# Sums of x taken with its additions and squares on ScalarE, delta*x on GpSimd, and the values' products of four key tiles in one run

## The chip, the cores and the metric

The kernel runs on one core of a Trainium2 chip. The metric is device time in microseconds (us) from start to end of the program, as the median of several runs. A core has five engines, each with its own queue that runs in the order written: TensorE (PE in the profile: matrix products; its loads of the stationary operand are shown as PEld), VectorE (DVE), ScalarE (ACT), GpSimd (POOL) and SyncE (SP), which here issues the DMA transfers. [...]

## The reference

Sixteen sequences of 512 tokens with 256 features pass three blocks; each block is put on a layer normalisation (mean and variance over the 256 features) and added to x:

```
x = x + attention(layernorm(x))     # RMS norm, 16 heads of 16, causal softmax, output projection, plus the normed x
x = x + experts(layernorm(x))       # base + shared low rank + top 2 of 6 low-rank experts
x = x + state_space(layernorm(x))   # conv, silu, delta = softplus(.), h = exp(A*delta)*h + delta*x*B, y = C.h, gate, projection
x = x + experts(layernorm(x))       # as before, once more
```

Everything is fp32. The recurrence runs over 512 steps for 256 features x 16 states of every sequence.

## The kernel before, in words

Each sequence stays in one tile `x` of 128 partitions (tokens) x 4 token tiles x 256. Its work is written as a list of 376 operations, each with an engine, an estimated cost, the buffers it reads and writes, and a function that issues the instructions. `Plan.order` (lines 126 to 220) simulates the engines with those costs while the program is being built, and picks on each engine the ready operation with the lowest priority number whose buffers are free. A priority is `STARTS[sequence] + TURNS[operation]`, two tables written out at the top. The order found is the order in which all queues are written, so operations of several sequences (four `x` tiles) are interleaved. `OVER` is by how many us a piece of work may overrun the moment for which an engine is kept free for the scores; `port=True` keeps big GpSimd operations and some VectorE operations apart in the plan.

The four stages of a sequence:

- `normalised` (476 to 497): for each of four token tiles, VectorE's `bn_stats` and `bn_aggr` (L481, L482) give mean and variance; GpSimd turns them into a scale and a shift in four small operations (L487 to L490); ScalarE applies them (L494). It is called four times a sequence: ahead of attention, routing, scan and the second routing. `turned` (L505, L508) transposes the result on TensorE, with a copy by ScalarE.
- `attention` (538 to 671): heads are worked in four groups `j` of four heads, two groups making a pair `i`. For each pair, scores of every query tile (L566, with the mask added by L568) only give the rows' maxima (VectorE, L637). The scores are then computed again for every key tile with the maxima folded in, ScalarE takes the exponential (L585) into `pt0` to `pt3`, and TensorE weighs the values with them (L590: four products of 32 columns each run side by side in the array). Scores for both go through `sc`, one buffer of four PSUM banks. The weighted values `av` are copied (L596), transposed back (L601) and divided (L608, L609).
- `routed` (674 to 763): routing of the experts in small VectorE operations, and products.
- `scan` (766 to 884): convolution (L780), gate, softplus to delta (L812), delta*x (L817, VectorE); delta and delta*x go out to DRAM (L816, L819) and come back spread over the states (L849); GpSimd multiplies by B (L856), ScalarE makes the decay (L861) in a PSUM bank, VectorE runs the recurrence (L864), GpSimd multiplies by C (L867), TensorE sums the states (L874).

`project` (515 to 530) ends each stage: products (L474), and VectorE adds two token tiles of the result to x in one instruction (L528). All PSUM tiles other than `sc` share one tag, `one`, with four banks; each of `pt0` to `pt3` has one buffer.

Of the kernel before, what the change touches and what calls it, by code (L numbers as in the profile page):

```python
# [21 lines left out]
OVER, CHANGE = 2.3, 97.0  # L22
STARTS = (
    0, 149, 234, 338, 413, 521, 619, 700, 790, 888, 996, 1074, 1174, 1263, 1369, 1447,
)
TURNS = (
    322, 924, 785, 870, 705, 84, 602, 525, 716, 736, 780, 829, 935, 688, 816, 888, 551, 888, 569, 780, 1037,
    1058, 780, 1053, 1052, 703, 823, 720, 796, 729, 794, 743, 758, 752, 822, 761, 826, 825, 945, 858, 844,
    656, 460, 479, 710, 820, 765, 711, 797, 755, 722, 823, 826, 738, 806, 840, 1808, 856, 863, 744, 849,
    851, 744, 788, 833, 754, 788, 766, 751, 859, 885, 1705, 883, 866, 807, 1037, 1066, 872, 1095, 1116, 757,  # L30
    814, 758, 845, 775, 829, 775, 854, 787, 878, 778, 819, 785, 833, 801, 850, 564, 392, 477, 669, 771, 810,
    720, 849, 837, 723, 824, 834, 729, 799, 814, 1625, 859, 798, 753, 898, 878, 758, 869, 924, 763, 873,
    814, 774, 828, 887, 1728, 845, 870, 913, 1017, 867, 1025, 795, 747, 619, 606, 834, 836, 824, 854, 204,
    875, 859, 701, 653, 760, 785, 601, 885, 649, 900, 844, 1052, 761, 625, 294, 465, 645, 644, 492, 604,
    701, 765, 811, 782, 660, 0, 531, 800, 645, 687, 566, 570, 613, 641, 518, 510, 470, 703, 660, 743, 1034,
    946, 605, 616, 676, 882, 619, 1044, 680, 1060, 712, 805, 957, 1000, 1101, 663, 941, 1101, 623, 890,
    1153, 849, 783, 616, 695, 622, 701, 684, 886, 650, 959, 803, 1136, 745, 727, 871, 1195, 973, 1019, 873,
    1211, 928, 818, 818, 937, 1046, 783, 1096, 904, 1208, 761, 767, 840, 962, 673, 1117, 931, 1159, 919,
    869, 880, 1059, 1081, 860, 1141, 944, 1257, 903, 867, 907, 1191, 989, 1264, 959, 1209, 1026, 890, 917,
    932, 1162, 952, 1293, 1071, 1366, 917, 930, 1018, 1268, 989, 1331, 1144, 1482, 1193, 1207, 930, 961,  # L40
    1168, 1480, 1042, 1195, 1009, 1344, 962, 968, 1052, 1231, 1060, 1264, 1093, 1321, 1019, 995, 969, 1128,
    1304, 1126, 1316, 1047, 1366, 973, 998, 1084, 1144, 1062, 1295, 1240, 1372, 1060, 993, 1019, 1122, 1311,
    1039, 1297, 1013, 1390, 1064, 1037, 1188, 1297, 1133, 1352, 996, 1349, 1058, 988, 1069, 1158, 1353,
    1153, 1350, 1021, 1424, 1076, 1045, 1055, 1230, 997, 1317, 1028, 1427, 999, 1130, 1032, 1059, 1037,
    1031, 1050, 1016, 1108, 1187, 528, 1091, 1082, 1153, 1067, 1132, 1266, 1209, 1446, 1077, 1275, 1141,
    1558, 1308, 1166, 904, 1004, 1071, 1242, 1188, 1479, 1564, 1511,
# [17 lines left out]
class Op:  # L64
    __slots__ = ("eng", "cost", "lat", "fn", "bufs", "after", "left", "seq", "turn", "num", "table", "load", "port", "then", "stage")


class Plan:
# [15 lines left out]
    def op(self, eng, cost, fn, r=(), w=(), lat=None, table=None, load=0.0, also=(), port=False):  # L84
# [29 lines left out]
        o.port, o.then, o.stage = port, None, self.stage  # L114
# [11 lines left out]
    def order(self):  # L126
# [4 lines left out]
        free, busy, table, link, port = dict(self.places), {}, None, 0.0, False  # L131
# [9 lines left out]
        while True:  # L141
            for eng, heap in ready.items():
# [28 lines left out]
                if o.table is not None:  # L171
                    cost += 1.3 * (o.table != table)
                    table = o.table
                if until is not None and self.wanted(o, what):
                    del kept[eng]
# [48 lines left out]
def tile_block(ctx: ExitStack, tc: tile.TileContext, a: dict, out: bass.AP):  # L224
# [198 lines left out]
    for name, k in (("st", 6), ("mv", 2), ("nm", 1), ("rs", 1)):  # L423
        sizes[name] = (3, [P, NT, k])
# [37 lines left out]
    def act(n):  # L462
        return 0.2 + n / 1200.0
# [12 lines left out]
    def normalised(x, eps, part, into):  # L476

        st, mv, rs, nm, xh = sbuf("st"), sbuf("mv"), sbuf("rs"), sbuf("nm"), sbuf("xh" + part)
        for t in range(NT):
            def stats(t=t):  # L480
                nc.vector.bn_stats(st()[:, t, :], x()[:, t, :])  # L481
                nc.vector.bn_aggr(mv()[:, t, :], st()[:, t, :])  # L482

            op("DVE", 0.6, stats, r=[(x, t)], w=[(st, t), (mv, t)])

        def scales():
            nc.gpsimd.tensor_scalar(rs()[:, :, 0], mv()[:, :, 1], eps, 1.0, ALU.add, ALU.mult)  # L487
            nc.gpsimd.tensor_tensor(rs()[:, :, 0], rs()[:, :, 0], neg_half, ALU.pow)  # L488
            nc.gpsimd.tensor_scalar(nm()[:, :, 0], mv()[:, :, 0], -1.0, 0.0, ALU.mult, ALU.add)
            nc.gpsimd.tensor_tensor(nm()[:, :, 0], nm()[:, :, 0], rs()[:, :, 0], ALU.mult)  # L490

        op("POOL", 1.65, scales, r=[mv], w=[rs, nm], port=True)
        for t in range(NT):
            op("ACT", act(256) + 0.18, lambda t=t: nc.scalar.activation(  # L494
                xh()[:, t, :], x()[:, t, :], AF.Identity, bias=nm()[:, t, 0:1], scale=rs()[:, t, 0:1]
# [454 lines left out]
```

## Time and profile before

| | |
|---|---|
| median of 3 runs | 2063.27 us (2061.38 to 2065.82) |
| profiled execution, its own time | 2066.51 us |
| its span, first to last instruction | 2064.7 us |
| TensorE clock granted, mean | 0.954 |
| busy: TensorE / VectorE / GpSimd / ScalarE | 1801.9 / 1513.4 / 1371.1 / 1194.0 us |
| DMA moved | 316.35 MB, mean 153 GB/s |

The profile comes from one execution. A group of instructions has a line, an engine, an operation, the tiles written and read, the shapes, a count, the busy time in us, the mean of one in ns, and the engine's idle time just before them with what ended it. Busy TensorE time counts overlapping products once, but does not show the pauses between runs of different shape. A wait is put down to the instruction that released it last.

### The profile page before, as it was taken

What the parts mean: (1) busy time and instruction counts of PE and PEld (TensorE: products, weight loads), DVE (VectorE), ACT (ScalarE), POOL (GpSimd) and SP (SyncE); (2) the same over time, 40 slices, a digit from 0 to 9 for tenths busy, and PEclk for the clock granted to TensorE, in tenths of its full rate; (3) what the DMA queues carried; (4) which work ended last, traced back from release to release, by engine and by line L of the source; (5) the groups of instructions that cost most, each with busy time, mean ns of one, the idle gap of its engine ahead of it and who ended that gap; (6) DMA issues with size and microseconds to landing.
All of it is one profiled execution on the core that took longest, in us unless ns stands there. A gap on an engine that the chain in (4) does not pass through costs nothing. (4 is left out here: it accounts for less than half of the span.)

```text
span 2064.7 us, 34733 instructions
## 1 busy us (share of the span) xinstructions
PE 1801.9 (87%) x13253; PEld 953.8 (46%) x13253; DVE 1513.4 (73%) x2479; ACT 1194.0 (58%) x1685; POOL 1371.1 (66%) x814
## 2 busy tenths in 40 slices
PE   4788789999999999999999999999999999996455
PEld 2244344555455454545455454545554454544123
DVE  4335677878788787878788787878788787876563
ACT  2236556565666757565666667575666766564431
POOL 3001784949587685859597785859596785848693
PEclk8789899999999999999999999999999999998766
DMA  3000956848494866847494867849493957747791
GB/s 93 1 1 22 216 122 155 197 127 210 109 233 109 216 164 167 205 137 191 110 231 100 225 153 175 204 120 212 110 231 95 228 143 186 183 125 183 186 222 31
DMA packets 113064, 316.35 MB, mean 153 GB/s; under 512 B 17809, under 2 KB 36610, under 8 KB 112898
## 3 DMA queue, kind: packets, MB, share of 16 engines
q1 hardware_dynamic: 112194, 313.99, 62.5%
q8 instruction: 105, 1.72, 0.4%
q14 instruction: 61, 0.50, 0.1%
q10 hardware_dynamic: 704, 0.14, 0.0%
HBM read 287.87 MB, written 26.21 MB: 152 GB/s over the span
## 5 line engine op out<-in xcount | busy, mean ns | idle before, releaser
L864 DVE TENSOR_TENSOR_SCAN dd<-one,dd 128x512 f32<-128x512 f32 x512 | 607.9, 1212 | 185.2 <-ACT one L861 88.3
L856 POOL TENSOR_TENSOR dd<-dd,bc 128x1024 f32<-128x1024 f32 x256 | 603.6, 2361 | 194.0 <-DMA dd<-drows 156.8
L867 POOL TENSOR_TENSOR dd<-dd,bc 128x1024 f32<-128x1024 f32 x256 | 601.9, 2358 | 86.2 <-DVE dd L864 80.4
L637 DVE TENSOR_REDUCE negm<-sc 128x4 f32<-128x512 f32 (+3 forms) x256 | 380.4, 1486 | 154.0 <-PE sc L568 153.7
L861 ACT ACTIVATE one<-dd,am 128x512 f32<-128x512 f32 x512 | 344.3, 689 | 249.4 <-DVE dd L864 108.9
L585 ACT ACTIVATE pt<-sc 128x2048 f32<-128x2048 f32 (+3 forms) x256 | 316.3, 1235 | 189.0 <-PE sc L568 187.8
L487 POOL TENSOR_SCALAR rs<-mv 128x4 f32<-128x4 f32 x64 | 12.3, 193 | 364.2 <-DVE mv L482 361.4
L566 PE MATMUL sc<-qm,kT 32*128 32x512 f32 (+3 forms) x2048 | 214.1, 488 | 37.8 <-ACT pt L585 28.4
L566 PE MATMUL sc<-kT,qT 32*128 32x128 f32 (+3 forms) x2048 | 217.0, 494 | 30.5 <-DVE negm L637 25.9
L568 PEld LDWEIGHTS <-identb 128*128 128x128 bf16 x2048 | 117.4, 98 | 232.4 <-issue 217.2
L874 PE MATMUL one<-dd,ysel 128*32 128x512 f32 x1024 | 172.7, 633 | 55.5 <-POOL dd L867 46.4
L590 PE MATMUL one<-pt,vv 128*32 128x512 f32 (+3 forms) x2048 | 191.6, 449 | 8.1 <-DVE dd L864 7.9
L566 PEld LDWEIGHTS sc<-qm,kT 32*128 32x128 f32 x2048 | 80.9, 185 | 181.5 <-ACT pt L585 120.4
L474 PE MATMUL one<-base,xtR 128*128 128x256 f32 x512 | 139.5, 395 | 18.6 <-DVE dd L864 18.0
L566 PEld LDWEIGHTS sc<-kT,qT 32*128 32x128 f32 x2048 | 82.0, 187 | 156.8 <-DVE negm L637 63.3
L494 ACT ACTIVATE xhR<-x,nm,rs 128x256 f32<-128x256 f32 x192 | 99.4, 588 | 53.2 <-POOL nm L490 53.1
L528 DVE TENSOR_TENSOR x<-one,x 128x512 f32<-128x512 f32 x128 | 86.4, 675 | 34.7 <-PE one L474 34.5
L474 PEld LDWEIGHTS one<-base,xtR 128*128 128x128 f32 x512 | 94.5, 194 | 36.8 <-DVE dd L864 21.5
L481 DVE BATCH_NORM_STATS2 st<-x 128x6 f32<-128x256 f32 x256 | 103.7, 405 | 4.8 <-DMA x<-in_x_dram 4.1
L568 PE MATMUL sc<-mask_q,identb 128*128 128x128 bf16 x1024 | 103.7, 225 | 0.0
L568 PE MATMUL sc<-mask_k,identb 128*128 128x128 bf16 x1024 | 102.8, 224 | 0.0
L505 PE MATMUL one<-ident,xhR 128*128 128x128 f32 x384 | 61.9, 290 | 35.2 <-ACT xhR L494 27.7
(132 smaller groups left out, 2449.4 us busy)
## 6 DMA issues: line engine op xcount, KB each, us to landing
dd<-drows SPq DMA_DIRECT2D x512, 512.0 KB
x<-in_x_dram SPq DMA_DIRECT2D x16, 512.0 KB
drows<-dt SPq DMA_DIRECT2D x32, 256.0 KB
drows<-sg SPq DMA_DIRECT2D x32, 256.0 KB
bc<-brows SPq DMA_DIRECT2D x16, 512.0 KB
out_dram<-x SPq DMA_DIRECT2D x16, 512.0 KB
brows<-few SPq DMA_DIRECT2D x16, 64.0 KB
wo<-in_Wo_dram SPq DMA_DIRECT2D x2, 256.0 KB
```

The lines of the kernel that those rows point to most:

```text
L474: nc.tensor.matmul(o[:, lo:hi], lhsT=lhsT, rhs=rhs, start=n == 0, stop=n == len(todo) - 1)
L481: nc.vector.bn_stats(st()[:, t, :], x()[:, t, :])
L566: nc.tensor.matmul(sc()[:, g, 0:n], lhsT=lhsT(g), rhs=rhs(g), start=True, stop=False)
L568: nc.tensor.matmul(sc()[:, g, at : at + P], lhsT=identb, rhs=mask, start=False, stop=True)
L585: o.then = op("ACT", act(G * n), lambda pt=pt, sc=sc, n=n: nc.scalar.activation(pt(), sc()[:, :, 0:n], AF.Exp), r=[sc], w=[pt], table="exp")
L590: nc.tensor.matmul(av()[rows(g), kt * P : T], lhsT=vals()[:, kt, G * j + g, :], rhs=pt()[:, g, :], start=kt == 0, stop=kt == NT - 1,)
L637: o.then = op("DVE", dve(G * n), lambda t=t, n=n, sc=sc, nm=nm, s=s: nc.vector.tensor_reduce(nm()[:, t, :, 1 - s, 0:1], sc()[:, :, 0:n], A ...
L856: op("POOL", pool(1024), lambda dd=dd: nc.gpsimd.tensor_tensor(dd()[:, :, 1, :], dd()[:, :, 1, :], both(0), ALU.mult), port=True, r=[(bc, ...
L861: op("ACT", act(512) + 0.07, lambda i=i, k=k, dd=dd, dec=dec: nc.scalar.activation(dec(), dd()[:, i, 0, :], AF.Exp, scale=am[:, k + 4 * i ...
L864: op("DVE", 1.22, lambda i=i, dd=dd, dec=dec: nc.vector.tensor_tensor_scan(dd()[:, i, 1, :], dec(), dd()[:, i, 1, :], 0.0, ALU.mult, ALU.a ...
L867: op("POOL", pool(1024), lambda dd=dd: nc.gpsimd.tensor_tensor(dd()[:, :, 1, :], dd()[:, :, 1, :], both(1), ALU.mult), port=True, r=[(bc, ...
L874: nc.tensor.matmul(sums()[rows(g), :], lhsT=ysel[:, m, :], rhs=four[g]()[:, g % 2, 1, :], start=m == 0, stop=m == 3)
```

## The change

The diff does five things.

1. `project` gets an option `more`, true for three of the four stages. Where it is set, VectorE adds each token tile on its own with `scalar_tensor_tensor`, which also writes the sum over the features into `sums`; the last stage of a sequence keeps the old addition.
2. `normalised` takes these sums where it is given them (three of its four calls): GpSimd makes the negative mean of them, ScalarE squares x minus the mean with the sum of squares as accumulator output (into the tile `xh`, which the normalised values overwrite later), GpSimd makes scale and shift in three small operations.
3. delta*x moves from VectorE to GpSimd.
4. The values' products of the four key tiles of a head group, before issued one by one after each exponential, are issued in one run after the last of them. The plan holds all four `pt` buffers from the scores on until that run.
5. The planner's costs are replaced by others (several given in the diff), `OVER` and `CHANGE` get other values, a cost of 0.2 us is left out where two 32-column runs follow each other, and both tables of priorities are replaced, so the order of all queues is another one. The list has 367 operations a sequence.

```diff
-OVER, CHANGE = 2.3, 97.0
+OVER, CHANGE = 1.8, 98.0
 STARTS = (
-    0, 149, 234, 338, 413, 521, 619, 700, 790, 888, 996, 1074, 1174, 1263, 1369, 1447,
+    0, 250, 450, 689, 961, 1201, 1411, 1675, 1928, 2203, 2451, 2680, 2957, 3175, 3503, 3764,
 )
...
+                if eng == "PE":
+                    cost -= 0.2 * (o.mode is not None and o.mode == mode)
+                    mode = o.mode
...
+        else:
+            op("POOL", 0.25, lambda: nc.gpsimd.tensor_scalar(
+                mv()[:, :, 0], sums()[:, :, 0], -1.0 / D, 0.0, ALU.mult, ALU.add
+            ), r=[sums], w=[(mv, 0)], port=True)
+            for t in range(NT):
+                op("ACT", act(256) + 0.2, lambda t=t: nc.scalar.activation(
+                    xh()[:, t, :], x()[:, t, :], AF.Square, bias=mv()[:, t, 0:1], accum_out=mv()[:, t, 1:2]
+                ), r=[(x, t), (mv, 0)], w=[(xh, t), (mv, 1 + t)], also=[into])
+
+            def scales():
+                nc.gpsimd.tensor_scalar(rs()[:, :, 0], mv()[:, :, 1], 1.0 / D, eps, ALU.mult, ALU.add)
+                nc.gpsimd.tensor_tensor(rs()[:, :, 0], rs()[:, :, 0], neg_half, ALU.pow)
+                nc.gpsimd.tensor_tensor(nm()[:, :, 0], mv()[:, :, 0], rs()[:, :, 0], ALU.mult)
...
-        op("PE", 0.66, turn, r=[xh], w=[one], also=[xt, *also])
+        op("PE", 0.57, turn, r=[xh], w=[one], also=[xt, *also])
...
-            op("DVE", dve(512), add, r=[one], w=[(x, t), (x, t + 1)])
+            def add_sum(t=t, one=one):
+                for i in range(2):
+                    nc.vector.scalar_tensor_tensor(
+                        x()[:, t + i, :], one()[:, i * D : (i + 1) * D], 1.0, x()[:, t + i, :], ALU.mult, ALU.add,
+                        accum_out=sums()[:, t + i, 0:1],
+                    )
...
-            o = op("PE", pe(n, 1, 0.09) + 0.45, run, r=reads, w=[sc], also=[into])
+            o = op("PE", pe(n, 1, 0.0) + 0.5, run, r=reads, w=[sc], also=[into])
...
+            pts = [sbuf(f"pt{kt}") for kt in range(NT)]
...
-                def weigh(kt=kt, pt=pt, av=av, j=j):
+            def weigh():
+                for kt in range(NT):
                     for g in range(G):
                         nc.tensor.matmul(
-                            av()[rows(g), kt * P : T], lhsT=vals()[:, kt, G * j + g, :], rhs=pt()[:, g, :],
+                            av()[rows(g), kt * P : T], lhsT=vals()[:, kt, G * j + g, :], rhs=pts[kt]()[:, g, :],
                             start=kt == 0, stop=kt == NT - 1,
                         )
-                op("PE", pe(n, 1, 0.1), weigh, r=[pt, vals], w=[av], also=[avs])
+            op("PE", 2.2 + 0.2, weigh, r=pts + [vals], w=[av], also=[avs], mode="columns")
...
-            op("DVE", dve(512) + 0.1, lambda e=e: nc.vector.tensor_tensor(dx()[:, e, :], dt()[:, e, :], xc()[:, e, :], ALU.mult),
+            op("POOL", pool(512), lambda e=e: nc.gpsimd.tensor_tensor(dx()[:, e, :], dt()[:, e, :], xc()[:, e, :], ALU.mult),
                r=[(dt, e), (xc, e)], w=[(dx, e)], port=True)
...
-        routed(x)
-        scan(b, x)
-        routed(x)
+        sums = routed(x, sums, True)
+        sums = scan(b, x, sums)
+        routed(x, sums, False)
```

Of the table `TURNS`, which has one number for each operation of a sequence, the change gives these typical values (before, then after): attention's scores 700 to 860, then 1290 to 1870; the first routing's operations 290 to 1050, then 130 to 1200; the scan's products by B 680 to 1190, then 1030 to 2140.

## The prediction

> **What bounds the kernel now.** I read first the page of the kernel before: engine totals and the row of slices.
>
> ```profile
> span 2064.7 us, 34733 instructions
> ...
> PE 1801.9 (87%) x13253; PEld 953.8 (46%) x13253; DVE 1513.4 (73%) x2479; ACT 1194.0 (58%) x1685; POOL 1371.1 (66%) x814
> ...
> PE   4788789999999999999999999999999999996455
> ...
> PEclk8789899999999999999999999999999999998766
> ```
>
> TensorE is the busiest, saturated from about 300 us to 1850 us, thin at both ends. Next, busy times by stretches of one sequence's length (the rows of the same kind lie 115.5 us apart: outputs leave at 400, 515, 630 ... 1786 us). Columns: length, then busy us of each engine, TensorE's clock, DMA share.
>
> ```profile
> 0.00:115.00 115.00, 70.23 (x442) 32.80 (x443) 42.27 (x85) 27.87 (x37) 15.53 (x32) 0.78 0.16 42
> 115.00:231.00 116.00, 97.36 (x748) 49.42 (x746) 53.66 (x101) 60.09 (x78) 19.92 (x16) 0.94 0.24 60
> 231.00:346.00 115.00, 101.77 (x760) 52.99 (x752) 82.88 (x121) 67.22 (x96) 76.83 (x43) 0.96 0.59 140
> ...
> 1501.00:1617.00 116.00, 109.11 (x832) 58.46 (x836) 93.61 (x152) 74.57 (x107) 85.56 (x51) 1.00 0.71 170
> ...
> 1848.00:1950.00 102.00, 67.98 (x368) 37.16 (x368) 62.92 (x94) 51.57 (x72) 79.87 (x41) 0.82 0.77 184
> 1950.00:2064.70 114.70, 53.06 (x187) 27.89 (x185) 54.60 (x96) 27.69 (x46) 74.82 (x39) 0.67 0.59 138
> ```
>
> In the middle a sequence takes 115.5 us, of which TensorE is busy 109, VectorE 94, GpSimd 86, ScalarE 75. The 6.5 us left to TensorE are not free: I took the start of every product in the trace, grouped them into runs of one line and shape, and set a run's end at its last start plus its columns at the pace seen inside runs. That splits the span into 1610 us of streaming, 1514 changes of array shape (32-row scores, full products, 32-column products) at 95 ns each (median gaps 94 to 96 ns for every pair of shapes) = 144 us, and about 290 us of waiting: 77 before 300 us, 110 after 1800 us, 99 between (6.6 per 100 us). Per middle sequence: 98.5 streaming, 9.0 changes, 8.0 waiting. So the middle is TensorE's. Who ends its waits from 300 to 1800 us (total us, times, longest):
>
> ```profile
> PE sc L566 <- ACT pt L585: 18.3, 64, 0.4
> PE one L474 <- DVE dd L864: 16.7, 12, 1.4
> PE one L645 <- DVE dd L864: 9.2, 13, 0.9
> PE one L590 <- DVE dd L864: 7.4, 13, 0.6
> PE one L505 <- DVE dd L864: 6.6, 13, 0.5
> ```
>
> The last four, 40 us, have nothing to do with the scan's data: the scan reads a decay out of one of the four `one` banks of PSUM, and a product waits for that bank. PSUM banks are the second limit.
>
> The prices come from the groups kept apart by shape (busy us, mean ns, then idle before):
>
> ```profile
> L856 POOL TENSOR_TENSOR dd<-dd,bc 128x1024 f32<-128x1024 f32 x256 | 603.6, 2361 | 194.0 <-DMA dd<-drows 156.8 <-PE one L474 14.3 <-PE one L645 8.0
> L481 DVE BATCH_NORM_STATS2 st<-x 128x6 f32<-128x256 f32 x256 | 103.7, 405 | 4.8 <-DMA x<-in_x_dram 4.1
> L494 ACT ACTIVATE xhR<-x,nm,rs 128x256 f32<-128x256 f32 x192 | 99.4, 588 | 53.2 <-POOL nm L490 53.1
> L528 DVE TENSOR_TENSOR x<-one,x 128x512 f32<-128x512 f32 x128 | 86.4, 675 | 34.7 <-PE one L474 34.5
> L482 DVE BATCH_NORM_AGGREGATE mv<-st 128x2 f32<-128x6 f32 x256 | 46.6, 182 | 8.9
> L817 DVE TENSOR_TENSOR sg<-dt,xc 128x512 f32<-128x512 f32 x32 | 25.9, 809 | 8.6 <-ACT dt L812 8.6
> ```
>
> [...] L817 (both in SBUF) takes 809 ns against 675 for L528 (one in PSUM)[...]. [...] The trace's loads take 1283 ns.
>
> **The change part by part.** Sums are against the profiled execution: span 2064.7, its time 2066.5, 3.2 above the median of 2063.3; I carry the difference to the median.
>
> *Merged values' products.* Three of four separate L590 runs go from each of 64 head groups. Taking those 192 out of the recorded order leaves 1325 changes of shape for 1514: 189 x 0.095 = -18 us on the bounding engine, -1.1 a sequence. Streaming stays. The second effect: the bank `av` is now held from the first run of L590 to the end of its copy L596, 10.47 us on average; with one run it is 2.13 (1280 columns, two passes) + about 1.0 from run to copy + 0.58 = 3.7. That frees 4 x 6.8 = 27 us a sequence of 4 x 115.5 = 462 bank-us, 6%. Worth between 0 and the 40 us above; I take -15. The new wait: the run waits for the fourth exponential, with all of TensorE's queue behind it, and the next group's first scores wait until it has freed `pt0`. Scores hold their one buffer for 1165 of the 1500 middle us, so 22% is slack, and the other pair's maxima (L637) can use it; while the long run goes, TensorE works anyway. I take 0, with the uncovered case below.
>
> *Statistics.* 48 of 64 normalisations lose 4 x (405 + 182) ns: -112.7 us of VectorE. 96 additions of 675 ns become two of 256 elements with an accumulator. L780's form takes 748 ns at 512, so 748 - 256/0.96 = 0.48 at 256; the accumulator is between 0 and 0.18 (the smallest VectorE instructions), I take 0.06: 2 x 0.54 - 0.675 = +0.41, x 96 = +39. With delta*x gone (-26) VectorE drops by 100, 6.2 a sequence (94 to 88). ScalarE gains 192 squares, nearest L494 at 588 ns, upper end 0.77; at 0.65 +125, 7.8 a sequence (75 to 82). A table set without squares would add up to 48 x 1.28 = 62 to it; ScalarE would still have some 30 us a sequence. GpSimd has four small operations as before. None bounds; directly 0.
>
> *delta*x on GpSimd.* 32 x half of 2361 = +38 us, 2.4 a sequence (86 to 88). Behind it stand L856 and L867, for which the scans wait; its store on SP's queue stands ahead of the fetches L849. GpSimd has 27 us of slack a sequence: 0 in the middle.
>
> *Where the cover is gone: the tail.* After the last exponential (1864 us) 197 us follow with one sequence's work left. A normalisation's chain changes by: addition +0.4, two statistics -1.2, GpSimd's mean +0.3, four squares +2.4, so +2, and one more turn in GpSimd's queue of 0 to 2.4. Three of them and two delta*x (+0.4 each and a turn): +7 to +18; I take +9.
>
> *Order.* All priorities are replaced. The new costs sit on this trace: scores of 512 columns cost 1.35 in the new plan and 1.48 in the old, and the trace gives 0.93 + 0.24 + two changes = 1.36. Four transposes 0.57 for 0.66; the trace 0.46 + 0.1. The queues run in written order, so gaps are laid where they now belong. I read priorities by phase: before, attention stands near 800 and the scan near 1030 with sequences 98 apart (2.3 ahead); after, 1490 and 1800 with 250 apart (1.2 ahead), and the first routing far ahead at about 700. GpSimd's first L856 is at 215 us, 81 after the first attention's end; earlier scans fill the start. The waits that order can reach are 77 + 99 + 110. Bounds: -90 (a third of them) to +40. I take -36: about 12 at the start, 24 in the middle (1.7 a sequence), nothing at the tail, where the serial chain rules.
>
> Sum: -18 - 15 + 9 - 36 = -60; 2063 - 60 = 2003 us.
>
> **Rivals.** *Only the changes of shape.* Banks and order give nothing, the tail costs 9: -9 to -30, 2033 to 2054, centre 2045. For it: 93% use of TensorE's time in the middle is hard to better. Against: the 40 us of bank waits. *The score chain becomes the bound (slower).* If each merged run starts late and nothing fills the single `sc` buffer, every one of 4 per sequence keeps it idle 2.13 + 0.19 + about 1 = 3.4 us: 13.6 on 25.9 idle. Half of the present idle is only TensorE being elsewhere, 13; so the chain needs 89.7 + 13 + 13.6 = 116.3, plus queueing. It decides when more than about 4 us per merged run stay uncovered; at 5.0 the period is 118.5 to 119, 14 x 3.3 = +46, 2100 us. For it: today's next first exponential follows 1.6 to 3.5 us after the fourth in half of the joints. Against: the gap to beat includes q scores that are independent. *The order gains all*: -18 - 40 - 90 + 9 = 1925.
>
> **Numbers.** The likeliest case (1960 to 2032) 0.60; only shapes (2032 to 2059) 0.20; more gain, under 1960, 0.03; within 0.2% (4 us, about what a measurement of this kernel can tell) 0.03; slower 0.14, of which a third ends below 2070. So faster 0.83, same 0.03, slower 0.14. 1960 to 2070 leaves out 0.03 and about 0.09.
>
> **What would show it.** TensorE's changes of shape near 1325 and its middle waiting below 8 us a sequence; L590's runs of four key tiles at about 2.1 us; waits "PE one ... <- DVE dd" under 25 us; outputs 112 to 114 us apart; VectorE near 1415, ScalarE near 1320, GpSimd near 1410; squares near 0.65 us without more table loads; GpSimd's first big product before 200 us. Wrong if the first exponential of a group waits for the values' products and outputs are 117 us or more apart, or if the time after the last exponential grows well over 206 us.

## The result, and the profile after

The changed kernel takes 2127.62 us (2121.08 to 2135.48), the kernel before 2064.55 us in the same session: ratio 1.031, 95% interval 1.027 to 1.035. It is slower by 63 us; the forecast was 2003 us, faster. The profiled execution of the changed kernel took 2121.08 us, its span is 2119.3 us, 54.6 longer than the span before.

The page of the changed kernel: span, engine totals, two rows of the 40 slices.

```profile
span 2119.3 us, 35012 instructions
...
PE 1800.9 (85%) x13253; PEld 979.2 (46%) x13253; DVE 1400.3 (66%) x2351; ACT 1292.8 (61%) x2077; POOL 1410.8 (67%) x846
...
PE   4678888999989998998999999998999998986544
...
PEclk8779999999999999999999999999999999998756
```

The engine totals are those forecast (VectorE 1415, ScalarE 1320, GpSimd 1410), and TensorE is busy as long as before, 1801 us. But between 300 and 1850 us its row, before a string of nines, now has eights. Outputs leave at 383, 502, 619, 739 ... us, 119.3 apart where it was 115.5.

The same stretches of the changed kernel, one period of 119 us each and the end (length, then busy us of TensorE, its loads, VectorE, ScalarE and GpSimd, granted clock, DMA share, GB/s):

```profile
0.00:119.00 119.00, 70.83 (x461) 34.39 (x465) 42.17 (x85) 32.18 (x40) 15.53 (x32) 0.80 0.16 40
119.00:238.00 119.00, 99.11 (x776) 52.54 (x771) 46.97 (x94) 55.72 (x85) 15.90 (x15) 0.90 0.17 41
...
1553.00:1672.00 119.00, 110.93 (x816) 60.22 (x808) 84.31 (x143) 78.70 (x127) 85.34 (x51) 0.94 0.66 158
1918.00:2020.00 102.00, 55.64 (x260) 32.14 (x252) 52.61 (x106) 47.59 (x90) 74.96 (x44) 0.74 0.70 169
```

In a middle period TensorE is busy 111 of 119 us (109 of 116 before), VectorE, ScalarE and GpSimd 79 to 85, and TensorE's clock stands at 0.94, where the kernel before had 1.00 there.

Split as in the forecast, TensorE's span is now 1607 us of streaming (1610 before), 1318 changes of array shape at 95 ns (1514 before, so 18.6 us less), and 365 us of waiting (287 before). Streaming is counted at full pace, so what a lower clock costs is counted as waiting here. Streaming and shapes gain 21, waiting loses 78. By place: 79 us of waiting before 300 us (77), 164 between 300 and 1800 (99), 122 after (110). The middle is where it was lost; by the profile alone, TensorE is idle for 128 us of it (88 before). Who ends TensorE's waits there, in the changed kernel (us in all, times, longest):

```profile
PE sc L603 <- ACT pt L623: 95.2, 78, 2.3
PE sc L603 <- DVE qm L690: 10.1, 12, 0.8
PE one L529 <- ACT xhR L518: 4.7, 11, 0.7
PE one L702 <- DVE dd L904: 4.0, 11, 0.4
PE one L630 <- DVE dd L904: 3.2, 9, 0.4
```

The first row was 18.3 us before, with a longest wait of 0.4. The scores wait for an exponential to leave the single buffer `sc`. The waits for PSUM banks behind the recurrence (DVE dd, 40 us before) have nearly gone: 9.9 us with two smaller rows.

The new operations, as groups of the changed kernel (busy us, mean ns, then idle before):

```profile
L507 ACT ACTIVATE xhR<-x,mv 128x256 f32<-128x256 f32 x192 | 95.1, 497 | 89.3 <-POOL mv L503 89.3
L507 ACT ACTIVATION_READ_ACCUMULATOR xhR<-x,mv 128x1 f32 x192 | 36.0, 187 | 0.0
L558 DVE SCALAR_TENSOR_TENSOR x<-one,x 128x256 f32<-128x256 f32 x192 | 72.7, 416 | 55.7 <-PE one L480 55.7
L558 DVE DVE_READ_ACCUMULATOR x<-one,x 128x1 f32 x192 | 15.9, 83 | 0.0
L503 POOL TENSOR_SCALAR mv<-sums 128x4 f32<-128x4 f32 x48 | 9.3, 193 | 249.7 <-DVE x L558 249.7
L857 POOL TENSOR_TENSOR sg<-dt,xc 128x512 f32<-128x512 f32 x32 | 40.5, 1266 | 146.3 <-ACT dt L852 146.3
```

A square costs 497 + 187 = 684 ns on ScalarE, an added token tile 416 + 83 = 499 ns on VectorE: near the 650 and 540 of the forecast (whose 0.96 elements per ns on VectorE is also what L637 shows in the kernel before: 684 ns for 512 elements, 2285 for 2048). What had not been priced is that engines stop in their queues for these operations: in the whole run GpSimd stood 250 us at the mean and 146 us at delta*x (before, 364 us at the scales of L487).

### The profile page after: what moved, and what is told of

It reads as the page before. It is cut to its first block, busy times and chain, and to the rows that moved or that the text cites. A ratio compares the mean times of both kernels' runs of the same rounds, so it can differ in the third digit from the quotient of the medians.

```text
span 2119.3 us, 35012 instructions
## 1 busy us (share of the span) xinstructions
PE 1800.9 (85%) x13253; PEld 979.2 (46%) x13253; DVE 1400.3 (66%) x2351; ACT 1292.8 (61%) x2077; POOL 1410.8 (67%) x846
## 5 line engine op out<-in xcount | busy, mean ns | idle before, releaser
L603 PE MATMUL sc<-qm,kT 32*128 32x512 f32 (+3 forms) x2048 | 224.9, 511 | 133.1 <-ACT pt L623 113.4
L603 PEld LDWEIGHTS sc<-qm,kT 32*128 32x128 f32 x2048 | 85.2, 195 | 233.0 <-ACT pt L623 165.0
L503 POOL TENSOR_SCALAR mv<-sums 128x4 f32<-128x4 f32 x48 | 9.3, 193 | 249.7 <-DVE x L558 249.7
L630 PE MATMUL one<-pt,vv 128*32 128x512 f32 (+3 forms) x2048 | 168.5, 473 | 3.5 <-DVE dd L904 3.2
L507 ACT ACTIVATE xhR<-x,mv 128x256 f32<-128x256 f32 x192 | 95.1, 497 | 89.3 <-POOL mv L503 89.3
L857 POOL TENSOR_TENSOR sg<-dt,xc 128x512 f32<-128x512 f32 x32 | 40.5, 1266 | 146.3 <-ACT dt L852 146.3
L630 PEld LDWEIGHTS one<-pt,vv 128*32 128x32 f32 x2048 | 63.3, 117 | 100.6 <-issue 79.3
L558 DVE SCALAR_TENSOR_TENSOR x<-one,x 128x256 f32<-128x256 f32 x192 | 72.7, 416 | 55.7 <-PE one L480 55.7
L605 PE MATMUL sc<-mask_k,identb 128*128 128x128 bf16 x1024 | 108.1, 232 | 0.0
L570 POOL TENSOR_TENSOR x<-x,bo 128x1024 f32<-128x1024 f32 x32 | 75.5, 2361 | 44.1 <-ACT xhR L518 29.7
```

The source lines that it names most:

```text
L603: nc.tensor.matmul(sc()[:, g, 0:n], lhsT=lhsT(g), rhs=rhs(g), start=True, stop=False)
L605: nc.tensor.matmul(sc()[:, g, at : at + P], lhsT=identb, rhs=mask, start=False, stop=True)
L630: nc.tensor.matmul(av()[rows(g), kt * P : T], lhsT=vals()[:, kt, G * j + g, :], rhs=pts[kt]()[:, g, :], start=kt == 0, stop=kt == NT - 1,)
```

## The experiments

Each ratio is against runs of the kernel before on the same chip in the same session. The letters of the theories are set anew in each group.

### The parts one by one, in the order of the kernel before

In this group A is that the joined run takes from TensorE the work that stood between the scores; B is that the new order is what loses. The order recorded before was kept in all four, and only what is issued at a place was changed.

Values' products kept back until the fourth exponential, or until the tile that they read is needed again:

```diff
-                def weigh(kt=kt, pt=pt, av=av, j=j):
+                def weigh(kt=kt, pt=pt, av=av, j=j, late=late):
+                    late.append((kt, pt))
+                    held[kt] = late
+                    if kt == NT - 1:
+                        flush(late, av, j)
```

> The kernel before with its order kept; only the values' products are kept back on TensorE's queue until the last key tile's (or until the tile of weights they read is about to be overwritten), so they run together. Theory A (these products were what TensorE did while ScalarE read the scores, and keeping them back leaves it waiting): 2095 to 2135 us, waits of scores for the exponentials well over 60 us in the middle instead of 18. Theory B (the loss comes from the new order of all queues, the merging is a gain): 2040 to 2060 us, because some 150 changes of array shape at 95 ns are saved.

Measured: 2185.03 us, ratio 1.059 (1.057 to 1.061): slower as A says, and 50 us beyond A's range. TensorE's changes of shape fell to 1325, as forecast of the merged run, and yet it lost 121 us. TensorE's first wait in the middle of this run:

```profile
PE sc L571 <- ACT pt L583: 93.9, 110, 2.0
```

With nothing but the products moved, the scores' waits for exponentials rise from 18.3 to 93.9 us, almost the 95.2 of the change. So that new wait is made by the joined run; it is 76 of the 121 us. What stood between the scores can be seen in two timelines (start, length, engine and line, idle time before it), of the kernel before and of the change:

```profile
706.41 0.40 PE L568 MATMUL sc<-mask_k,identb 128*128 128x128 bf16 x4
706.74 0.85 PE L590 MATMUL one<-pt,vv 128*32 128x384 f32 x8
707.92 0.50 PE L566 MATMUL sc<-qm,kT 32*128 32x128 f32 x8 [0.33 <-ACT pt L585]
```

```profile
480.83 0.40 PE L605 MATMUL sc<-mask_k,identb 128*128 128x128 bf16 x4
482.34 1.19 PE L603 MATMUL sc<-qm,kT 32*128 32x384 f32 x8 [1.11 <-ACT pt L623]
```

Before, values' products follow the scores of one key tile (which end with the mask), then the next scores. In the change 56 of the 95.2 us of these waits begin right behind the mask: nothing stands between.

New statistics alone (additions with sums, mean by GpSimd, squares by ScalarE at the place of GpSimd's scales):

```diff
+                nc.gpsimd.tensor_scalar(mv()[:, :, 0], sums[0][:, :, 0], -1.0 / D, 0.0, ALU.mult, ALU.add)
+                for t in range(NT):
...
+                    nc.scalar.activation(junk, x()[:, t, :], AF.Square, bias=mv()[:, t, 0:1], accum_out=mv()[:, t, 1:2])
```

> The kernel before with its order kept; only the statistics are changed: sums with the additions, mean on GpSimd, squares on ScalarE, all issued where GpSimd's scales stood. Theories A and B: 2055 to 2075 us, no bound is touched. Theory C (the longer chain of each normalisation, through GpSimd twice and ScalarE twice, delays what feeds TensorE): 2085 us or more.

Measured: 2167.36 us, ratio 1.050 (1.048 to 1.052), 104 us lost, as theory C of this expectation has it. GpSimd's waits in the middle of this run, in the same columns:

```profile
POOL rs L494 <- ACT junk L493: 165.9, 37, 7.7
POOL mv L490 <- DVE x L543: 132.6, 13, 19.0
```

Before, GpSimd stopped once at a normalisation, 182.6 us in the middle. Now it stops for the additions and again for the squares, 298 us.

delta*x on GpSimd alone (the same call, `nc.gpsimd` for `nc.vector`):

> The kernel before with its order kept; only delta*x is issued on GpSimd at the same place. Theories A and B: 2060 to 2070 us. Theory C (GpSimd in series with the scan's feed): 2080 us or more.

Measured: 2063.40 us, ratio 0.9996 (0.9988 to 1.0004). No loss in this order, although GpSimd stands at delta*x for 151 us of the middle.

All three together, in the order before:

> The three parts together, in the order of the kernel before, so only the order of the queues differs from the kernel after. Theory A: 2100 to 2140 us, like the kernel after. Theory B: 2035 to 2070 us, 60 or more below the kernel after. Theory C: the sum of the losses of the two single runs, over 2100 us.

Measured: 2293.01 us, ratio 1.111 (1.109 to 1.113): 229 us, and 121 + 104 + 0 is 225. The losses add up. The order written for the changed program takes 165 of the 229 us back. B, that the new order is the loss, falls for the changed program; and in this order the forecast of 0 falls for two of the three parts.

### The parts undone, in the order of the change

If the joined run or the statistics were the loss in this order too, undoing one should give time back. Products of each key tile issued behind the next tile's scores where a PSUM bank was free:

```diff
-            op("PE", 2.2 + 0.2, weigh, r=pts + [vals], w=[av], also=[avs], mode="columns")
+            runs.append((op("PE", 2.2 + 0.2, None, r=pts + [vals], w=[av], also=[avs], mode="columns"), scores, piece, av))
...
+            for piece, kt in behind.get(i, []):
+                piece(kt)
```

> The kernel after with its order kept; only each key tile's values' products are taken out of the single run and issued on TensorE's queue behind the scores of the next key tile. Theory A (these products were what TensorE did while ScalarE read the scores): 2060 to 2090 us, the middle's waits of scores for exponentials fall from 95 to under 40 us, although 150 to 190 changes of array shape come back (+14 to +18). Theory B (the new order itself is what waits): 2125 to 2150 us, the waits stay and the changes of shape are added.

Measured: 2203.10 us, ratio 1.068 (1.066 to 1.071). Both theories missed; it is 75 us slower than the change. TensorE's first waits in the middle of this run:

```profile
PE sc L605 <- ACT pt L625: 63.4, 60, 2.0
PE sc L605 <- DVE negm L678: 48.9, 60, 1.6
```

The waits for exponentials fell from 95 to 63 us as A says, but scores that read row maxima now wait 48.9 us for VectorE, and the changes of shape are back at 1499. The order had been laid out for joined runs.

VectorE's statistics put back in place of GpSimd's mean, without squares, and then with the products apart as well:

> The kernel after with its order kept; only the statistics are as before (bn_stats and bn_aggr where GpSimd's mean stood, plain additions, no squares). If the new order has hidden the longer chain of the normalisation that cost 104 us in the old order: 2115 to 2150 us. If that chain still costs in the kernel after: under 2105 us.

> The two together in the order of the kernel after. Theory A with hidden statistics: the same as with the products apart alone, 2060 to 2100 us. If the statistics still cost: below 2050 us. Theory B: over 2115 us.

Measured: 2154.36 us, ratio 1.044 (1.042 to 1.046), and 2217.29 us, 1.074 (1.072 to 1.076). Undoing costs 27 and 90 us: the first is 4 us beyond the range for a chain that the new order hides, the second lies in B's range. In either direction, an operation changed or moved costs tens of us where the order of the queues was not made for it; only delta*x, in the old order, did not. A part alone in a foreign order therefore may overstate its own cost, and can't price the change.

### An order of its own for each program

So I looked for other starting times, priorities and weights for three programs, and ran one order of each. A is now that the loss is that of one poor order, B that it belongs to the operations. Only the two tables and the two weights change, here those of the changed program:

```diff
-OVER, CHANGE = 1.8, 98.0
+OVER, CHANGE = 1.89305, 1603.35
 STARTS = (
-    0, 250, 450, 689, 961, 1201, 1411, 1675, 1928, 2203, 2451, 2680, 2957, 3175, 3503, 3764,
+    0, 257, 364, 159, 882, 305, 573, 413, 1213, 736, 122, 1028, 607, 806, 989, 1490,
 )
```

> The changed program, every operation and cost as in the change, but with other starting times, turns and the two weights of the ordering, so that the same operations are issued in another order. Theory A (the 63 us are the order's: the changed program is not worse than the program before, but sits in an order that lets scores wait for exponentials): 2050 to 2085 us, at least 40 below the change, and TensorE's waits for exponentials ahead of scores fall well below the change's 95 us in 300 to 1800 us. Theory B (the loss belongs to the changed operations: with the values' products of four key tiles in one run nothing is left to put between scores, and the sums need GpSimd and ScalarE where VectorE alone did it): 2105 us or more, the waits for exponentials stay near 95 us.

> The program before, unchanged in its operations, with other starting times, turns and ordering weights, found in the same manner as those of the changed program in another order. Measures what a new order alone is worth to the program before. Theory A: about as much below 2064 us as the other order of the changed program comes below 2085, so that the two programs end within 20 us of each other. Theory B: 2035 to 2060 us, and 50 us or more below the changed program in its other order.

> The changed program's sums, squares on ScalarE and delta*x on GpSimd, but the values' products of each key tile apart again, in an order of its own. Theory A: like the changed program in its other order within 20 us. Theory B: the statistics cost what they cost (20 to 40 us over the program before in another order), the joined run the rest, so this stands between the two. If it is the fastest of the three, the joined run is the part that loses.

| program | other order, us | ratio to the kernel before |
|---|---|---|
| before | 2059.54 | 0.9995 (0.998 to 1.001) |
| change, products apart | 2092.78 | 1.014 (1.011 to 1.017) |
| change | 2105.49 | 1.020 (1.018 to 1.023) |

A different order gives the changed program 22 of its 63 us and the program before nothing. A falls: 46 us remain between the two where it allows 20. B fits better, though it wanted 50; 33 of the 46 come with the new statistics and delta*x, another 13 with the joined run. TensorE's waits at scores in 300 to 1800 us, first in the change in its other order, then with products apart:

```profile
PE sc L600 <- ACT pt L620: 86.0, 74, 2.0
```

```profile
PE sc L600 <- DVE negm L671: 59.2, 50, 2.2
PE sc L600 <- ACT pt L619: 19.5, 38, 0.8
```

The wait for exponentials follows the joined run: 95.2, 93.9 and 86.0 us in three orders with it, 18.3 and 6.6 in two orders of the program before, 19.5 in an order made for products apart (63.4 where they were put apart in a foreign order). But with products apart the scores wait 59.2 us for VectorE's row maxima instead, so at scores TensorE waits 79 us in all against 89 with the joined run, and 14 in the other order of the program before. These are single orders, and a better one may exist for each; an order alone moved the changed program by 22 us, so the split into 33 and 13 is not shown to be the operations' own.

### Does TensorE pay twice for its waits?

The clock of the middle had fallen. The profile's clock records of the changed kernel show 102.4 us at half clock between 300 and 1800 us, in 25 records of 3.4 or 6.8 us; in those of the kernel before none begins there. TensorE's timeline in the changed kernel (start, length, engine and line, idle before it and who ended that):

```profile
480.19 0.71 PE L603 MATMUL sc<-qm,kT 32*128 32x256 f32 x8 [1.52 <-ACT pt L623]
...
482.34 1.19 PE L603 MATMUL sc<-qm,kT 32*128 32x384 f32 x8 [1.11 <-ACT pt L623]
...
484.01 1.94 PE L914 MATMUL one<-dd,ysel 128*32 128x512 f32 x8
```

Two waits for exponentials, 2.6 us in 4, and right behind them a run of eight products takes 1.94 us; the same run takes 1.06 us at 526.77. A record of half clock reaches from 482.88 to 486.29 us and covers the slow run. No wait of the middle is longer than 2.3 us, and in the 3.4 us ahead of each of the 25 records, the length of the shorter ones, TensorE was busy for 31 to 52% of the time. Stretches as idle as these without a record behind them occur too, but not in step with the records, which all begin at multiples of 3.41 us from one another: of the 439 slices of that step in the middle the 25 idlest, busy for up to 51.6%, are those ahead of the records, and the others are busy for 52.3% or more (in the kernel before, all for 57.3% or more). Two traces don't show whether that is the condition.

The records can be set against the starts of the products. Inside a record the next product of a run follows at 1.9 times the usual distance (median; of 158 distances of 40 ns and more, 133 are over 1.5 times the usual), outside 17 of 4115 distances are over 1.5 times. The steps from one product's start to the next that lie wholly in a record take TensorE 84.6 us, and the same steps take about 47 us elsewhere. So TensorE loses some 38 us of the middle to its clock, where the kernel before loses none.

The test fills the waits. Ahead of scores that had waited over 0.8 us (121 places), useless bf16 products of a mask cover about 70% of the wait:

```diff
+                n = FILL.get(turn, 0) if live[i] < banks["one"][0] else 0
+                if n:
+                    idle = ps.tile([P, 512], F32, tag="one", name="one", bufs=banks["one"][0])
+                    for k in range(n):
+                        nc.tensor.matmul(idle[:, 0:P], lhsT=identb, rhs=mask_k, start=k == 0, stop=k == n - 1)
```

> The change in its own order, with useless bf16 products of a mask (128x128 by 128 columns, some 55 ns each) put in front of the scores that waited over 0.8 us in the change's trace, 121 places, about 70% of each wait, some 105 us of added TensorE work; nothing reads them. Theory C (the waits cost twice: while TensorE waits its clock falls to half, and the next products run at half pace): the time at half clock in 300 to 1800 us falls from 102 us to under 40 and the run gets faster although TensorE does 105 us more, 2080 to 2110 us. Rival D (the waits are the loss by themselves, half clock only goes with them): the run stays or gets slower, 2120 to 2160 us, since the products only stand where TensorE waited or delay what follows.

Measured: 2113.30 us, ratio 1.025 (1.023 to 1.027), 14 us less than the change (12 by the ratios) although TensorE runs 1941 more products. From the page of this run and its waits in the middle, the products and what they wait for themselves:

```profile
L976 PE MATMUL one<-mask_k,identb 128*128 128x128 bf16 x1941 | 130.6, 221 | 48.4 <-DVE dd L921 43.5
```

```profile
PE one L976 <- DVE dd L921: 41.3, 25, 2.3
PE sc L619 <- ACT pt L640: 21.3, 44, 0.9
```

Time at half clock in the middle fell to 30.7 us, and what TensorE loses in these records from 38 to 12 us. The direction is C's; the size misses C's range by 3 us: 14 us where 18 to 48 were expected, with 41 us of waiting for banks that the filler brought along. So the lowered clock is a part of the 63 us: 12 to 14 came back, net of the filler's own waits. How much of TensorE's 38 us reaches the time of the whole kernel is not shown. The kernel with filled waits is still 51 us slower than the kernel before.

The other orders say the same of the clock: in the middle 119.5 us are at half clock with the change in its other order and 85.3 with products apart, but none in either order of the program before.

### What the statistics lose by

Theory L: the added work on ScalarE. Theory K: the longer chain from the additions to the normalised values. Both runs keep the order before. First the squares besides the old statistics, with nobody reading their sums; then the squares of the new statistics on VectorE:

```diff
+                    nc.scalar.activation(junk, x()[:, t, :], AF.Square, accum_out=spare[:, t : t + 1])
```

```diff
-                    nc.scalar.activation(junk, x()[:, t, :], AF.Square, bias=mv()[:, t, 0:1], accum_out=mv()[:, t, 1:2])
+                    nc.vector.scalar_tensor_tensor(
+                        junk, x()[:, t, :], mv()[:, t, 0:1], x()[:, t, :], ALU.add, ALU.mult, accum_out=mv()[:, t, 1:2]
+                    )
```

> The kernel before with its own statistics and order, and besides them 192 squares with accumulator on ScalarE at the place of GpSimd's scales in three of four normalisations, whose sums nothing reads. They wait only for x. ScalarE has the added work of the change (192 x 0.68 = 131 us), and no operation waits for it except by standing behind it in ScalarE's queue. Theory L (the statistics cost what they cost by ScalarE's load: exponentials, copies and decays stand behind 2.7 us of squares): 2120 us or more, more than half of the 104 us that the squares cost in this order. Theory K (they cost by the longer chain: additions, mean, squares, scales, normalised values one after the other through three engines): under 2090 us.

> The kernel before in its order with sums taken by the additions and the squares issued at the same place as in the squares alone, but by VectorE (scalar_tensor_tensor with accumulator) instead of ScalarE. The chain addition, mean on GpSimd, squares, scales is the same, ScalarE has no added work; VectorE loses the old statistics and gains 192 x about 0.5 us of squares, and its queue waits for GpSimd's mean. Theory L: within 25 us of the program before, up to 2090 us. Theory K: 2120 us or more, since the chain is as long, and VectorE now stands waiting in it.

Measured: 2083.98 us, ratio 1.011 (1.008 to 1.013), and 2126.69 us, 1.031 (1.029 to 1.033). ScalarE's 131 us of added work, in the middle of its queue, cost 21 us; the chain without that work, with VectorE now standing in it, costs 63. K holds in this order. Since GpSimd stops twice in the chain, the next theory (G) was that its stop for the mean holds up the products by B and C behind it. VectorE makes the mean instead, behind each addition:

```diff
-            op("POOL", 0.25, lambda: nc.gpsimd.tensor_scalar(
-                mv()[:, :, 0], sums()[:, :, 0], -1.0 / D, 0.0, ALU.mult, ALU.add
-            ), r=[sums], w=[(mv, 0)], port=True)
+            op("POOL", 0.25, lambda: None, r=[sums], w=[(mv, 0)], port=True)
...
+                nc.vector.tensor_scalar(sums()[:, t : t + 2, 0], sums()[:, t : t + 2, 0], -1.0 / D, 0.0, ALU.mult, ALU.add)
```

> The squares alone in the order before (2167 us), but the negative mean is no longer made by GpSimd: VectorE makes it in two small instructions behind its additions (one for each addition of two token tiles). GpSimd keeps only its three operations for scale and shift, as many stops in its queue as in the kernel before. Theory G (the statistics lose by GpSimd's queue, which now stops twice at each normalisation, once for the additions and once for the squares, with products by B and C behind): under 2120 us, half or more of the 104 us come back. Rival K (the chain of squares on ScalarE and back to GpSimd is what loses): 2145 us or more.

> As the squares on VectorE in the order before (2127 us), and the mean on VectorE too: nothing on ScalarE, GpSimd stops once as in the kernel before. Theory G: 2055 to 2085 us. Rival K: 2105 us or more.

> The change in its own order, with the negative mean made by VectorE behind each addition and GpSimd's operation for it left out; nothing else moves. Theory G: 2085 to 2115 us, since GpSimd stood 250 us over the run at this operation. Rival (in the order of the change GpSimd's stop for the mean is no loss, because its queue has slack there, and the scores' waits for exponentials rule): 2120 to 2132 us.

> The changed program in the other order (2105 us) with the negative mean on VectorE. Theory G: 2065 to 2095 us. Rival: 2100 to 2112 us.

| mean on VectorE in | us | ratio to the kernel before | without it, us |
|---|---|---|---|
| the squares alone, order before | 2206.25 | 1.068 (1.063 to 1.072) | 2167.36 |
| the squares on VectorE, order before | 2162.44 | 1.048 (1.047 to 1.050) | 2126.69 |
| the change | 2155.95 | 1.045 (1.043 to 1.047) | 2127.62 |
| the change, other order | 2119.92 | 1.027 (1.025 to 1.029) | 2105.49 |

All four became slower than the same program without it, by 14 to 39 us. The group of the new instruction, in the change with the mean on VectorE:

```profile
L560 DVE TENSOR_SCALAR sums<-sums 128x2 f32<-128x2 f32 x96 | 79.1, 824 | 3.3
```

Two columns take 824 ns. The timeline of that run shows why, VectorE and then GpSimd:

```profile
702.31 0.17 DVE L560 TENSOR_SCALAR sums<-sums 128x2 f32<-128x2 f32 x1
...
882.08 0.70 DVE L560 TENSOR_SCALAR sums<-sums 128x2 f32<-128x2 f32 x1
...
880.40 2.36 POOL L906 TENSOR_TENSOR dd<-dd,bc 128x1024 f32<-128x1024 f32 x1
```

At 702 us no large GpSimd product runs, and it takes 0.17 us. At 882 us one runs until 882.76, and the small instruction ends at 882.78. In the whole run the 44 that start beside no such product all take 169 to 171 ns; 49 of the 52 others end within 40 ns of that product's end. What the two engines contend for, the trace doesn't show. So these four runs added 79 to 100 us to VectorE and don't tell on G. The last run leaves the mean out with no instruction in its place; ScalarE's square takes sum - 256 x by its own scale and bias:

```diff
-                    xh()[:, t, :], x()[:, t, :], AF.Square, bias=mv()[:, t, 0:1], accum_out=mv()[:, t, 1:2]
+                    xh()[:, t, :], x()[:, t, :], AF.Square, bias=sums()[:, t, 0:1], scale=-float(D), accum_out=mv()[:, t, 1:2]
```

> The change in its own order without any mean ahead of the squares: ScalarE squares (sum - 256 x) by scale and bias of the activation, so GpSimd doesn't stop for the additions; the factors go into its operations for scale and shift, four in one stop as in the kernel before. No engine has an added instruction: it leaves the 0.8 to 1.0 us instruction of VectorE out that spoilt the runs with the mean on VectorE. Theory G (GpSimd's second stop at each normalisation costs the change some of its 63 us): 2085 to 2115 us. Rival (GpSimd's stop is in its slack there; the stop at the squares takes its place): 2118 to 2135 us.

Measured: 2130.24 us, ratio 1.033 (1.030 to 1.036), the change itself. GpSimd's waits in the middle, of the change and then of this run:

```profile
POOL sg L857 <- ACT dt L852: 118.5, 13, 9.3
POOL mv L503 <- DVE x L558: 84.0, 22, 6.2
...
POOL rs L512 <- ACT xhR L507: 29.9, 21, 2.2
```

```profile
POOL sg L856 <- ACT dt L851: 116.6, 13, 9.1
POOL rs L510 <- ACT xhR L505: 109.6, 16, 8.6
```

84.0 + 29.9 us at two stops became 109.6 at one, and both are less than the 182.6 us of the kernel before. GpSimd has that slack, and G falls. The trace speaks against K in the change as well: in its own order the last normalised values come 7.6, 8.4 and 7.3 us after the last addition (routing, scan, second routing; medians over twelve sequences), against 9.9, 6.6 and 8.4 in the kernel before. The new order keeps the chain about as short as it was.

What stays open is the 33 us that the new statistics and delta*x cost in orders of their own. GpSimd's stop for the mean is excluded by a run in the order of the change, the chain's length only by the times just given; the squares' work explains up to 21 of it if its cost in the old order carries over, which was not tried. Nor was delta*x put back on VectorE in the new order, though GpSimd stops there for some 9 us in every sequence (118.5 us over 13); in the old order it stopped there longer, 151 us, and lost nothing. One lead: the run with products apart, which has these 33 us, loses 33 us of TensorE's time in records of half clock, and the program before loses none there. Whether its waits for row maxima pull the clock down, and why they arise, was not tested.

## Why the prediction was wrong

**Changes of shape, right.** 1318 against 1325 forecast, 18.6 us against 18, and streaming stayed. The gain is real and is lost elsewhere.

**PSUM banks, right and more.** Waits behind the recurrence went from 40 to 10 us, 30 gained where 15 was taken.

**The joined run's new wait, taken at 0: the first step that failed.** The reasoning was that scores have 22% slack, that the other pair's maxima can use it, and that "while the long run goes, TensorE works anyway". The slack of the score buffer was real: a sequence holds it 90.5 us as before (89.7). But the queue is in order, and the single products that stood between one tile's scores and the next had been the filling. In their place TensorE stands: its waits go from 18.3 to 95.2 us. The forecast looked for the new wait at the joined run; it came at the scores ahead of it. The rival for this case, the score chain as the bound, gave a period of 118.5 to 119 and 2100 us, with 0.14 for any slower result. Its sum doesn't hold: 89.7 + 13 and four times 5.0 is 122.7, and 118.7 belongs to 4.0 uncovered us a run. That the measured period is 119.3 is luck: the score buffer's idle time rose only from 25.9 to 28.6 us a sequence, and behind the fourth key tile it is 0.7 us a run, not 5.0. The loss is TensorE standing in front of the buffer.

**TensorE's clock, not in the sum at all.** No term of the forecast lets the middle's clock of 1.00 fall. The new waits brought it to 0.94 in a middle period, and TensorE loses some 38 us to it there.

**Statistics, taken at 0: the second.** Instruction times and engine totals were right, and no table set was in the way beyond small change (75 loads of 1283 ns for 67). What costs is mostly not work. In the old order it was 104 us, of which 21 are ScalarE's work; in orders of their own the statistics and delta*x are left with 33. The slack per engine that the forecast summed up ("30 us a sequence") says nothing on whom an in-order queue makes wait.

**delta*x, taken at 0.** Right in the old order, 0.9996. Not settled in the new. One reading of the profile was wrong on the way: the 809 ns of L817 is a mean of unlike cases (in the kernel before; shortest, median, longest in ns):

```profile
L817 DVE TENSOR_TENSOR sg<-dt,xc x32: 657/691/2890, 201.4 to 1932.9; 128x512 f32<-128x512 f32 x32
```

Thirty of the 32 take 657 to 693 ns, like the 675 of L528, and no large GpSimd product runs beside them; the two that meet one take 2545 and 2890 ns and end 0.55 us after it. So in these two cases the two engines do get in each other's way, but 809 against 675 doesn't measure it.

**Order, taken at -36: the third, and the largest single term.** The forecast read that "the new costs sit on this trace" as a gain against the kernel before. The order did gain 165 us, but against what the three edits do in the old order (2293), so it paid back a loss that the forecast had put at nothing. Against the kernel before no gain is seen: another order of that program gave 0.9995. None of the sub-steps came: waiting in the middle rose from 6.6 to 11 us per 100, the first 300 us kept theirs (79 for 77), and GpSimd's first large product came at 230 us, not before 200.

**Tail, taken at +9.** From the start of the last exponential to the end of the span it is 201.8 us against 200.5, +1 (the forecast's 197 is too low: 2064.7 - 1864 is 200.7); by TensorE's waiting after 1800 us +12.

In sum, for the span: -18.6 for shapes, -2.3 for streaming, +65 for the middle's waits, +11.5 for the end's, +1.6 for the start's, together +57 where the spans differ by 54.6. Such a split can't tell the rest, and where a run's end is set otherwise some 15 us go from streaming to waiting. The lowered clock is inside the +65: some 38 us of TensorE's time.

## What to carry to other kernels

A small operation that stands between two dependent ones on a saturated in-order engine is its filling: before runs are joined to save changes of shape, look at what waits will stand bare, and price them at the place where the engine stops, not at the operation that moved. When an edit comes with a new order, price the edit in the old order and the order on the old program: a gain that only pays back the edit is none. Where new waits stand bare, read the granted clock too, since the waits can be paid a second time at a lower pace (here some 38 us of TensorE's time in the middle). Slack in busy time is no permission to move work; ask at which instruction the queue will stop and what stands behind.

## What the runs showed of the hardware

- TensorE fell to half clock in the middle of a busy kernel with no wait longer than 2.3 us: in the 3.4 us ahead of each of the 25 records it was busy for 31 to 52% of the time. Inside a record products follow each other at 1.9 times the usual distance. Filling such waits with useless products took the middle from 102.4 to 30.7 us at half clock and made the whole kernel 14 us faster.
- An accumulator output costs 187 ns on ScalarE and 83 ns on VectorE, as an instruction of its own.
- A `tensor_scalar` of two columns on VectorE takes 0.17 us alone and up to 2.3 us (the longest of 14 between 600 and 900 us) when it starts beside a large GpSimd product: in 49 of 52 cases it ended with that product; the additions (`scalar_tensor_tensor` from PSUM) right ahead of it kept their 0.42 us.
- delta*x of 128x512, both inputs in SBUF, takes 1266 ns on GpSimd and 691 ns (median) on VectorE. The two of 32 that met a large GpSimd product there took 2.5 and 2.9 us.
